# Attention's product of softmax weights and rows of h, in three float32r passes for one graph of each pair

## The chip, the cores and the metric

The kernel runs on one core of one Trainium2 chip. The metric is the device time of one execution in microseconds (us); lower is better. The kernel before takes 2072.49 us, the median of 4 runs (2069.57 to 2074.41).

## The reference

There are 64 graphs of 256 nodes with 256 features, each with its own 256x256 adjacency matrix. Layer 0 is a gated graph network: three rounds of message passing and a GRU cell. Layer 1 is a graph attention layer. Both are preceded by a layer norm and a ReLU and followed by a residual sum.

```python
# layer 0
h = jnp.maximum(_layernorm(x), 0.0)
for i in range(3):
    m = einsum('bnd,de->bne', h, weight[i]);  aggr = einsum('bst,bsd->btd', A, m)
    h = _gru_cell(aggr, h, w_ih, w_hh, b_ih, b_hh)
x = x + h
# layer 1
g = jnp.maximum(_layernorm(x), 0.0)
h = einsum('bnd,od->bno', g, W)
e = (h @ a_left)[:, :, None] + (h @ a_right)[:, None, :]
e = where(adj == 0, NEG_INF, where(e > 0, e, 0.2 * e))
x = x + einsum('bij,bjd->bid', softmax(e, -1), h)
```

The kernel multiplies the softmax weights by g first and applies W afterwards; the two orders give the same result. The "rows of h" of the change are these rows g (buffer `hb` in the kernel).

## The kernel before, in words

The graphs go in 32 pairs (`G` = 2). A pair's state is held transposed, 128 features x 512 nodes (two graphs side by side) in each of two buffers. A pair runs through three GRU rounds and then through attention.

**Numbers in two forms.** Most products are made in float32r, the fast reduced form of float32 on TensorE, in three passes. `split` (lines 470 to 478) makes three float32r buffers out of one float32 buffer: one ScalarE copy with a scale (line 473) and two VectorE operations (lines 474 and 476). The first two passes go into a PSUM bank, ScalarE multiplies the bank in place by `SPLIT + 1`, and the third pass is added on top. In the gates the first two passes are line 498, the scaling line 512, the third pass line 503; in attention's product with W ("project") both matmul parts are line 778 and the scaling is line 783. Attention's first product, softmax weights by rows of `hb` ("mix", line 770), is made in plain float32 instead: four matmuls with 256 columns for each graph, which the trace records as eight MATMULs.

**Attention, for all pairs but the last** (`far`): rows of scores are masked, their exponentials taken (line 753), the weights turned by the DMA engines into `pT` (line 536 joins the two halves on ScalarE: "p copy"), mixed on TensorE into the bank `pg`, split ("c0", "c1"), projected, and added to the residual (line 787). The last pair has an attention of its own (lines 793 and after), row block by row block.

**Buffers.** Every tile comes from a class of equal slots: 25 `full` (float32), 32 `round` (float32r) of 128x512, 8 PSUM banks and a few small ones.

**The order of the work.** A planner (`Plan.run`) writes out one static order for each engine before anything runs. Each operation has an engine, an estimated time for which it occupies the engine, a latency, and the buffers that it reads and writes. The planner walks through time: of all operations whose inputs and buffers are there it places the one that can start first, and among equals the one with the smallest priority value. That value comes from the deadline of the pair, less the latencies of what follows, less an entry of the table `LEAD` (in ns), which moves an operation by name ahead (positive) or back (negative). `WINDOW` = 4 pairs may be under way at once. Names get the prefix "first", "late" or "last" for the pairs 0, 30 and 31. At run time each engine goes through its list in order, and semaphores hold it where an input is not there yet.

TensorE therefore finds work of two or three pairs in its list, interleaved: gates of one pair beside the products of another's attention.

Of the kernel before, what the change touches and what calls it, by code (L numbers as in the profile page):

```python
# [10 lines left out]
F32 = mybir.dt.float32  # L11
# [3 lines left out]
AF = mybir.ActivationFunctionType  # L15
ALU = mybir.AluOpType
# [8 lines left out]


LEAD = {
    "w load": 17000, "w d": -3000, "G": 4000, "first A": 32000, "first in 0 eps": 5000, "first nh 1 topF": 4000,
    "first lo 1": -14000, "in 0 eps": -2000, "in 0 relu": 71000, "in 1 stats": -3000, "in 1 relu": 57000,
    "h0 0": 3000, "h1 1": -8000, "prop 0": 4000, "g0 0": -24000, "g0 1": -19000, "prop 1": 30000, "g1 1": 23000,  # L30
    "r 0 topT": 2000, "ni 0 topF": -18000, "ni 0 scale": -10000, "u add 0": 1000, "z 0 topF": -114000,
    "z 0 rest": 11000, "z 0": 55000, "d add 0": -14000, "r 1 topT": -55000, "r 1 rest": -22000, "nh 1 rest": 5000,
    "ni 1 topF": -23000, "z 1 topF": -162000, "z 1 scale": -94000, "z 1": 51000, "d sub 1": -3000,
    "d add 1": -14000, "back copy 1": -43000, "mask 0": -6000, "mid 1 stats": -52000, "max 1": -19000,
    "c0 0": 12000, "late r 0 rest": -15000, "late nh 0 rest": -22000, "late r 1 topF": 16000,
    "late r 1 rest": -3000, "late nh 1 topF": 15000, "late ni 1 topF": -8000, "late project 1 scale": -47000,
    "last in 0 stats": 10000, "last in 1 relu": 16000, "last h0 1": -30000, "last h1 1": 21000,
    "last r 0 topF": -2000, "last nh 0 rest": 2000, "last z 0 rest": -36000, "last lo 0": -47000,
    "last back 1": -34000, "last nh 0 of 0 topF": 20000, "last ni 1 of 0 rest": 12000,
    "last nh 0 of 1 topF": -17000, "last nh 1 of 1 topF": 21000,  # L40
}


# [164 lines left out]
def tile_gated_gnn_then_gat(  # L208
# [39 lines left out]
    nc = tc.nc  # L248
    P = 128
    B, N, D = x.shape  # L250
    L = weight.shape[0]
    NB = N // P
    DB = D // P
    G = 2
# [20 lines left out]
    ALL = (0, 1)  # L275
    ONE = (0,)

    def parts(b):
        return b.t[:, :GN].rearrange("p (k d) -> p k d", k=2)
# [3 lines left out]
    def pe(name, n, fn, **kw):  # L283
        return plan.op(name, "PE", n, n + 220, fn, **kw)

    def act(name, n, fn, **kw):
        plan.op(name, "ACT", n, n + 170, fn, **kw)

    def dve(name, n, fn, **kw):
        plan.op(name, "DVE", n, n + 160, fn, **kw)  # L290

    def dve2(name, n, fn, **kw):
        plan.op(name, "DVE", n, n + 160, fn, port=True, **kw)
# [8 lines left out]
    MM, TR, PROP, PASS = 432, 109, 120, 232  # L302
    A512, V512, S512, VP256, C512 = 475, 605, 660, 392, 522
    LINE, SPREAD = 4600, 4600
    SPLIT = 4096.0
    C = 1.0 / SPLIT
    BELOW = 1.0 - C / 2
# [162 lines left out]
    def split(name, v, bank=False):  # L470

        v0, v1, vd = Buf("round"), Buf("round"), Buf("round")
        act(name + " 0", A512 if bank else C512, lambda: nc.scalar.activation(v0.t, v.t, AF.Copy, scale=BELOW), r=[(v, ALL)], w=[(v0, ONE)])  # L473
        (dve if bank else dve2)(name + " 1", V512, lambda: nc.vector.tensor_sub(v1.t, v.t, v0.t.bitcast(F32)),  # L474
                                r=[(v, ALL), (v0, ONE)], w=[(v1, ONE)])
        dve2(name + " d", V512, lambda: nc.vector.scalar_tensor_tensor(  # L476
            vd.t, v1.t.bitcast(F32), -SPLIT, v0.t.bitcast(F32), op0=ALU.mult, op1=ALU.add),
            r=[(v0, ONE), (v1, ONE)], w=[(vd, ONE)])
        return v0, v1, vd
# [5 lines left out]
    def columns(part):  # L485
        return slice(part[0] * N, (part[-1] + 1) * N)
# [47 lines left out]
    def join(name, src, dst, order="b j n"):  # L534

        act(name, 1065, lambda: nc.scalar.copy(  # L536
            dst.t.bitcast(U16).rearrange("p (j n b) -> p j n b", j=2, b=2),
            src.t.bitcast(U16).rearrange(f"p ({order}) -> p j n b", j=2, b=2)), r=[(src, ALL)], w=[(dst, ALL)])

    def planes(b):  # L540
        return lambda rows: b.t[rows].bitcast(U16).rearrange("p (b k n) -> p b k n", b=2, n=P)
# [27 lines left out]
    def pair(p):  # L569
# [5 lines left out]
        A = [Buf("round") for _ in range(G)]  # L575
        h = [Buf("full") for _ in range(G)]
        hi, lo = [Buf("round") for _ in range(G)], [Buf("round") for _ in range(G)]
        for g in range(G):
            dve2("A", 340, lambda g=g: nc.vector.tensor_scalar(A[g].t, ADJ[p][g].t, 0.0, None, op0=ALU.not_equal),
                r=[(ADJ[p][g], ALL)], w=[(A[g], ONE)])  # L580
# [3 lines left out]
                r=[(h[g], ALL), (hi[g], ONE)], w=[(lo[g], ONE)])  # L584
# [21 lines left out]
        for i in range(L):  # L606
            last = i == L - 1
# [23 lines left out]
            for part in [(0,), (1,)] if apart else [ALL]:  # L631
                cols, of = columns(part), " of %d" % part[0] if apart else ""
                for db in range(DB):
                    plan.due = 1000.0 * SLOT * (3 * p + 2 * i) + (8000.0 * part[0] if apart else 0)
                    d = hT[db]
                    pr = gate(f"r {db}{of}", db, [("hh", hs), (i, gs)], tops, True, part=part)
                    r_, z_, u = Buf("full"), Buf("full"), Buf("full")
                    act(f"r {db}{of}", fit(575, part), lambda b=r_, k=pr, db=db, cols=cols: nc.scalar.activation(  # L638
                        b.t[:, cols], k.t[:, cols], AF.Tanh, bias=b_rz[:, db : db + 1], scale=0.5),
                        r=[(pr, ONE), ("b_rz", ONE)], w=[(r_, ONE)])  # L640
# [12 lines left out]
                        r=[(pz, ONE), ("b_rz", ONE)], w=[(z_, ONE)])  # L653
# [10 lines left out]
            if not last:  # L664
                hi, lo = [Buf("round") for _ in range(DB)], [Buf("round") for _ in range(DB)]
            for g, db in [(g, db) for g in range(G) for db in range(DB)] if apart else []:
                hn = Buf("bank")

                def back(g=g, db=db, hn=hn):
# [6 lines left out]
                    r=[(hn, ALL)], w=[(XR[g], ALL)])  # L676
            for db in range(0 if apart else DB):
# [12 lines left out]
                if last:  # L690
                    for g in range(G):
                        v = lambda b, g, db: b.t.rearrange("p (g k f) -> p g k f", g=G, k=NB)[:, g]
                        dve_(f"res {db}", 335, lambda g=g, db=db, b=XR[g], hn=hn, v=v: nc.vector.tensor_add(
                            parts(b)[:, :, ts(db, P)], parts(b)[:, :, ts(db, P)], v(hn, g, db)), r=[(hn, ALL)], w=[(XR[g], ALL)])
                else:
                    act(f"hi {db}", C512, lambda b=hi[db], hn=hn: nc.scalar.copy(b.t, hn.t), r=[(hn, ALL)], w=[(hi[db], ONE)])
                    dve_(f"lo {db}", V512, lambda b=hi[db], c=lo[db], hn=hn: nc.vector.tensor_sub(c.t, hn.t, b.t.bitcast(F32)),  # L697
                         r=[(hn, ALL), (hi[db], ONE)], w=[(lo[db], ONE)])
# [3 lines left out]
        hb, sc, pm_ = ([Buf("full") for _ in range(G)] for _ in range(3))  # L702
# [5 lines left out]
        for g in range(G):  # L708
# [4 lines left out]
            for nb in range(NB):  # L713
                for n in range(2):
                    c = 12 + n * NB + nb
# [3 lines left out]
                        r=[(hb[g], (nb,)), ("va", ONE)], w=[(sm, (c,)), (sc[g], (nb,))])  # L719
# [3 lines left out]
            if p < NPAIR - 1:  # L723
# [3 lines left out]
                    r=[(sm, (14, 15))], w=[(line, ONE)])  # L727
# [13 lines left out]
            for nb in range(NB):  # L741
# [4 lines left out]
                r=[(A[g], ONE), (sc[g], ALL)], w=[(pm_[g], ALL)])  # L746
            dve(f"max {g}", 610, lambda b=pm_[g], sm=sm: nc.vector.tensor_reduce(sm.t[:, 0:NB], parts(b), AX.X, ALU.max, negate=True),
                r=[(pm_[g], ALL)], w=[(sm, ONE)])
# [9 lines left out]
        for g in range(G if far else 0):  # L758
            sm = sms[g]
            dve("recip", 70, lambda sm=sm: nc.vector.reciprocal(sm.t[:, 8 : 8 + NB], sm.t[:, 4 : 4 + NB]),  # L760
                r=[(sm, (1,))], w=[(sm, (2,))])
            pT, pg, pv = Buf("full"), Buf("bank"), Buf("bank")
            rs = Buf("full")
            dma_turn(f"p turn {g}", pm_[g], pT, [((rs, ALL), planes(rs), slice(None))])
            join(f"p copy {g}", rs, pT)

            def mix(g=g, pT=pT, pg=pg):
                for db in range(DB):
                    for jb in range(NB):
                        nc.tensor.matmul(pg.t[:, ts(db, N)], parts(hb[g])[:, jb, ts(db, P)],  # L770
                                         pT.t.rearrange("p (i j n) -> p i j n", j=NB, n=P)[:, :, jb, :], start=(jb == 0), stop=(jb == NB - 1))

            pe(f"mix {g}", 4 * MM, mix, r=[(pT, ALL), (hb[g], ALL)], w=[(pg, ONE)])
            cs = split(f"c{g}", pg, True)

            def project(js, first, cs=cs, pv=pv):
                for n, (ib, db, j) in enumerate((ib, db, j) for ib in range(NB) for db in range(DB) for j in js):
                    nc.tensor.matmul(pv.t[:, ts(ib, D)], cs[j].t[:, db * N + ib * P : db * N + (ib + 1) * P],  # L778
                                     fac["W"][:, j, db, :], start=(first and n == 0), stop=True, skip_group_check=True)

            pe(f"project {g}", 8 * PROP, lambda project=project: project((0, 1), True),
               r=[(cs[0], ONE), (cs[1], ONE), ("facW", ((0, 0), (1, 0)))], w=[(pv, ONE)])
            act(f"project {g} scale", A512, lambda pv=pv: nc.scalar.activation(pv.t, pv.t, AF.Copy, scale=SPLIT + 1.0), w=[(pv, ONE)])
            pe(f"project {g} rest", 4 * PROP, lambda project=project: project((2,), False),
               r=[(cs[2], ONE), ("facW", ((0, 1), (1, 1)))], w=[(pv, ONE)])
            for nb in range(NB):
                dve(f"out {g}", VP256, lambda b=XR[g], nb=nb, pv=pv, sm=sm: nc.vector.scalar_tensor_tensor(
                    parts(b)[:, nb, :], pv.t[:, ts(nb, D)], sm.t[:, 8 + nb : 9 + nb], parts(b)[:, nb, :],
                    op0=ALU.mult, op1=ALU.add), r=[(pv, ONE), (sm, (2,))], w=[(XR[g], (nb,))])
            dma("store", 256, lambda g=g, b=XR[g]: nc.sync.dma_start(rows(out, G * p + g), parts(b)), r=[(XR[g], ALL)])  # L790


        for g, ib in [(g, ib) for g in range(G) for ib in range(NB)] if not far else []:
            stagger(g)
            sm, name, row, total = sms[g], f" {g} {ib}", (sms[g], (("row", ib),)), (sms[g], (("total", ib),))
            pt, pT, pg, ag, pv = Buf("bank"), Buf("full"), Buf("bank"), Buf("full"), Buf("bank")
# [4 lines left out]
                r=[row], w=[total])  # L801
# [17 lines left out]
            def project(ag=ag, pv=pv):  # L819
# [6 lines left out]
                r=[(pv, ONE), total], w=[(XR[g], (ib,))])  # L826
# [39 lines left out]
```

## Time and profile before

| what | value |
|---|---|
| median of 4 runs | 2072.49 us |
| the profiled execution, its own time | 2073.07 us |
| its span in the profile | 2071.3 us |
| granted TensorE clock | 0.998 |
| busy: TensorE / weight load / VectorE / ScalarE / GpSimd | 99% / 82% / 84% / 85% / 8% |
| mean DMA rate | 117 GB/s |

"PE" is TensorE's matmul row, "PEld" its weight loads, "DVE" VectorE, "ACT" ScalarE, "POOL" GpSimd, "SP" the engine that issues the DMAs. A group row gives line, engine, operation, destination and source tiles, shape, the count, the busy time, and the mean duration of one instruction in ns; what follows the last bar is the idle time of the engine ahead of these instructions and what ended it. A duration holds the whole instruction; queued instructions of one engine overlap a little, so the step from one start to the next is shorter. In the chain of waits a piece is a start, a length and what ran; the length is the step by which the chain moved on.

### The profile page before, as it was taken

The page shows a single profiled execution, that of the slowest core. Times are in us where ns is not written, and L with a number is a line of the kernel's source. Part 1 is how long each engine was busy: PE and PEld are TensorE (multiplying, and loading weights), DVE is VectorE, ACT ScalarE, POOL GpSimd, SP SyncE. Part 2 cuts the span into 40 slices and gives each one's busy share as a digit, 9 for nine tenths or more (in the row PEclk, how much of TensorE's full clock was granted, in tenths as well). Part 3 has the DMA queues.
Part 4 walks back from the last instruction along what each step waited for, and adds up shares of the span by engine and source line. Part 5 has one row for each costly group of instructions (what it writes and reads, how often), then busy time and mean ns, then how long its engine had stood idle before and what let it go on. Part 6 is the DMA issues. An engine that isn't in the chain of part 4 may idle for free.

```text
span 2071.3 us, 31400 instructions
## 1 busy us (share of the span) xinstructions
PE 2048.3 (99%) x9957; PEld 1693.9 (82%) x9957; DVE 1738.2 (84%) x3892; ACT 1761.8 (85%) x3049; POOL 157.7 (8%) x198
## 2 busy tenths in 40 slices
PE   8999999999999999999999999999999999999997
PEld 6888887888888888888888888888888888888887
DVE  7778888888888888888788888788888888888877
ACT  6788888888888888988888888888888888888876
POOL 1000000000000000000000000000000000000000
PEclk9999999999999999999999999999999999999999
DMA  4257677667776566866677766778766778666632
GB/s 121 62 100 131 128 136 107 119 108 133 138 119 112 114 122 128 140 112 109 110 135 130 126 114 115 113 130 143 110 114 119 121 128 143 108 116 111 111 70 57
DMA packets 742918, 241.52 MB, mean 117 GB/s; under 512 B 666704, under 2 KB 742752, under 8 KB 742752
## 3 DMA queue, kind: packets, MB, share of 16 engines
q1 hardware_dynamic: 742720, 239.51, 66.0%
q8 instruction: 78, 1.28, 0.3%
q14 instruction: 88, 0.72, 0.2%
q10 hardware_dynamic: 32, 0.01, 0.0%
HBM read 61.09 MB, written 16.84 MB: 38 GB/s over the span
## 4 chain that ended last, share of the span: by engine, by line
PE 86%; DVE 5%; DMA 4%; ACT 3%; issue 1%; SPq 0%; ACTq 0%; DVEq 0%
PE bank L498 46%; PE bank L503 23%; PE bank L619 8%; PE bank L778 4%; DMA full<-full 4%; PE bank L770 4%; DVE round L474 1%; PE bank L447 1%; ACT full L564 1%; ACT full L536 1%; DVE round L476 1%; ACT bank L512 0%; ACT round L473 0%; DVE full L745 0%; DVE full L657 0%
## 5 line engine op out<-in xcount | busy, mean ns | idle before, releaser
L498 PE MATMUL bank<-round,fac 128*128 128x512 f32 (+1 forms) x2328 | 617.1, 393 | 0.3
L498 PE MATMUL bank<-round,fac_hh 128*128 128x512 f32 (+1 forms) x2328 | 613.1, 396 | 0.0
L498 PEld LDWEIGHTS bank<-round,fac 128*128 128x128 f32 x2328 | 433.2, 188 | 105.8 <-DVE round L474 2.8
L498 PEld LDWEIGHTS bank<-round,fac_hh 128*128 128x128 f32 x2328 | 430.6, 188 | 96.7
L512 ACT ACTIVATE bank<-bank 128x512 f32<-128x512 f32 (+1 forms) x582 | 334.1, 577 | 95.5 <-PE bank L498 88.0
L536 ACT COPY full<-full 128x1024 uint16<-128x1024 uint16 x308 | 358.6, 1165 | 31.8 <-DMA full<-full 24.4
L503 PE MATMUL bank<-round,fac 128*128 128x512 f32 (+1 forms) x1164 | 356.5, 392 | 0.0
L503 PE MATMUL bank<-round,fac_hh 128*128 128x512 f32 (+1 forms) x1164 | 353.8, 394 | 1.1 <-ACT bank L512 1.1
L476 DVE SCALAR_TENSOR_TENSOR round<-round,round 128x512 fp32r<-128x512 f32 x446 | 305.9, 688 | 8.0
L503 PEld LDWEIGHTS bank<-round,fac 128*128 128x128 f32 x1164 | 215.1, 188 | 55.0 <-ACT bank L512 5.5
L558 POOL TENSOR_TENSOR small<-small,nhalf 128x2 f32<-128x2 f32 x128 | 123.8, 975 | 1690.3 <-DVE small L556 1613.4
L503 PEld LDWEIGHTS bank<-round,fac_hh 128*128 128x128 f32 x1164 | 205.9, 188 | 46.0 <-ACT bank L512 8.9
L474 DVE TENSOR_TENSOR round<-bank,round 128x512 fp32r<-128x512 f32 x254 | 173.8, 686 | 60.2 <-ACT round L473 56.9
L619 PEld LDWEIGHTS bank<-round,round 128*128 128x128 f32 x1536 | 208.7, 191 | 14.2 <-DVE round L697 0.3
L619 PE MATMUL bank<-round,round 128*128 128x256 f32 x1536 | 215.7, 284 | 0.1
L643 DVE SCALAR_TENSOR_TENSOR full<-full,bank 128x512 f32<-128x512 f32 (+1 forms) x194 | 131.5, 678 | 54.4 <-ACT full L638 52.7
L648 ACT ACTIVATE full<-full,vec 128x512 f32<-128x512 f32 (+1 forms) x194 | 139.4, 719 | 41.9 <-DVE full L646 21.5
L651 ACT ACTIVATE full<-bank,b_rz 128x512 f32<-128x512 f32 (+1 forms) x194 | 132.7, 684 | 45.9 <-PE bank L503 44.5
L473 ACT ACTIVATE round<-bank 128x512 fp32r<-128x512 f32 x254 | 146.7, 592 | 28.7 <-PE bank L619 25.9
L657 DVE SCALAR_TENSOR_TENSOR full<-full,full 128x512 f32<-128x512 f32 (+1 forms) x194 | 130.4, 672 | 32.1 <-ACT full L651 31.9
L474 DVE TENSOR_TENSOR round<-full,round 128x512 fp32r<-128x512 f32 x192 | 130.7, 683 | 30.0 <-ACT round L473 27.6
L646 DVE TENSOR_TENSOR full<-full,bank 128x512 f32<-128x512 f32 (+1 forms) x194 | 131.0, 676 | 24.7 <-PE bank L503 17.3
(95 smaller groups left out, 2295.6 us busy)
## 6 DMA issues: line engine op xcount, KB each, us to landing
full<-full SPq DMA_DIRECT2D x492, 128.0 KB, 3.7
x<-in_x_dram SPq DMA_DIRECT2D x64, 256.0 KB, 3.2
adj<-in_adj_dram SPq DMA_DIRECT2D x64, 256.0 KB, 4.3
full<-in_x_dram SPq DMA_DIRECT2D x64, 256.0 KB, 3.3
full<-full SPq DMA_DIRECT2D x248, 64.0 KB, 2.5
out_dram<-full SPq DMA_DIRECT2D x62, 256.0 KB, 2.5
full<-line SPq DMA_DIRECT2D x62, 128.0 KB, 3.8
full<-full SPq DMA_TRANSPOSE x308, 3.2
```

The costliest lines, as they stand in the source:

```text
L473: act(name + " 0", A512 if bank else C512, lambda: nc.scalar.activation(v0.t, v.t, AF.Copy, scale=BELOW), r=[(v, ALL)], w=[(v0, ONE)])
L474: (dve if bank else dve2)(name + " 1", V512, lambda: nc.vector.tensor_sub(v1.t, v.t, v0.t.bitcast(F32)), r=[(v, ALL), (v0, ONE)], w=[(v1, ...
L476: dve2(name + " d", V512, lambda: nc.vector.scalar_tensor_tensor(vd.t, v1.t.bitcast(F32), -SPLIT, v0.t.bitcast(F32), op0=ALU.mult, op1=ALU ...
L498: nc.tensor.matmul(bank.t[:, cols], f(m, j, kb), b.t[:, cols], start=(first and n == 0), stop=True, skip_group_check=True)
L503: nc.tensor.matmul(bank.t[:, cols], f(m, 2, kb), s[kb][2].t[:, cols], start=False, stop=True, skip_group_check=True)
L512: act(name + " scale", fit(575 if "nh" in name else 515, part), lambda: nc.scalar.activation(bank.t[:, cols], bank.t[:, cols], AF.Identity ...
L536: act(name, 1065, lambda: nc.scalar.copy(dst.t.bitcast(U16).rearrange("p (j n b) -> p j n b", j=2, b=2), src.t.bitcast(U16).rearrange(f"p ...
L619: nc.tensor.matmul(pa.t[:, ts(g, N)], b, parts(A[g])[:, sb, :], start=(n == 0), stop=(n == len(terms) - 1))
L643: dve(f"u {db}{of}", fit(S512, part), lambda u=u, k=ph, b=r_, cols=cols: nc.vector.scalar_tensor_tensor(u.t[:, cols], b.t[:, cols], 1.0, k ...
L646: dve(f"u add {db}{of}", fit(V512, part), lambda u=u, k=pn, cols=cols: nc.vector.tensor_add(u.t[:, cols], u.t[:, cols], k.t[:, cols]), r=[ ...
L648: act(f"tanh {db}{of}", fit(615, part), lambda u=u, en=en, cols=cols: nc.scalar.activation(u.t[:, cols], u.t[:, cols], AF.Tanh, bias=b_i[: ...
L651: act(f"z {db}{of}", fit(575, part), lambda b=z_, k=pz, db=db, cols=cols: nc.scalar.activation(b.t[:, cols], k.t[:, cols], AF.Tanh, bias=b ...
```

## The change

For graph 0 of each pair from 0 to 30, the mix is made in three float32r passes like the other products. Both operands are split: `hb` into three buffers `w` (scaled by `C * BELOW`, one ScalarE and two VectorE operations), `pT` into three buffers `vs` (the same counts). Eight matmuls of 256 columns go into `pg`, ScalarE scales the bank, four more matmuls follow. Graph 1 keeps the four float32 matmuls, and the last pair is as before. The table `LEAD` is another one: 30 entries in place of 60, 16 names in both.

```diff
 LEAD = {
-    "w load": 17000, "w d": -3000, "G": 4000, "first A": 32000, "first in 0 eps": 5000, "first nh 1 topF": 4000,
-    ...
-    "last nh 0 of 1 topF": -17000, "last nh 1 of 1 topF": 21000,
+    "w load": 18000, "first h0 d": -14000, "first nh 1 topF": 3000, "first ni 1 topF": 11000, "in 0 stats": 5000,
+    "in 0 eps": 4000, "in 1 stats": 19000, "in 1 shift": -113000, "in 1 relu": 75000, "h0 1": -9000,
+    "nh 0 topF": 9000, "ni 0 topF": -33700, "ni 0 rest": -10000, "z 0 topF": -125000, "z 0 rest": 40000,
+    "d mul 0": 20000, "d add 0": 8000, "r 1 topT": -93000, "ni 1 topF": -33300, "z 1 topF": -182000,
+    "z 1 scale": -142000, "back copy 1": -41000, "mid 0 stats": -18000, "mid 1 stats": -102000, "c1 0": 72000,
+    "late nh 1 topF": 15000, "late back 0 gather": 15000, "late mix 0": -7000, "last in 1 stats": -18000,
+    "last back 1 of 0": 15000,
 }
...
+            def mix_in_three(first, cs, pg=pg):
+                for n, (db, jb, (w, v)) in enumerate((db, jb, c) for db in range(DB) for jb in range(NB) for c in cs):
+                    nc.tensor.matmul(pg.t[:, ts(db, N)], parts(w)[:, jb, ts(db, P)],
+                                     v.t.rearrange("p (i j n) -> p i j n", j=NB, n=P)[:, :, jb, :],
+                                     start=(first and n == 0), stop=True, skip_group_check=True)
...
-            pe(f"mix {g}", 4 * MM, mix, r=[(pT, ALL), (hb[g], ALL)], w=[(pg, ONE)])
+            if g > 0:
+                pe(f"mix {g}", 4 * MM, mix, r=[(pT, ALL), (hb[g], ALL)], w=[(pg, ONE)])
+            else:
+                w = [Buf("round") for _ in range(3)]
+                act(f"hb{g} 0", C512, lambda g=g, w=w: nc.scalar.activation(w[0].t, hb[g].t, AF.Copy, scale=C * BELOW),
+                    r=[(hb[g], ALL)], w=[(w[0], ONE)])
+                dve2(f"hb{g} 1", V512, lambda g=g, w=w: nc.vector.scalar_tensor_tensor(
+                    w[1].t, w[0].t.bitcast(F32), -SPLIT, hb[g].t, op0=ALU.mult, op1=ALU.add),
+                    r=[(hb[g], ALL), (w[0], ONE)], w=[(w[1], ONE)])
+                dve2(f"hb{g} d", V512, lambda w=w: nc.vector.tensor_sub(w[2].t, w[1].t.bitcast(F32), w[0].t.bitcast(F32)),
+                     r=[(w[0], ONE), (w[1], ONE)], w=[(w[2], ONE)])
+                vs = split(f"p{g}", pT)
+                pe(f"mix {g}", 8 * PROP, lambda cs=list(zip(w, vs)), mix=mix_in_three: mix(True, cs[:2]),
+                   r=[(b, ONE) for b in w[:2] + list(vs[:2])], w=[(pg, ONE)])
+                act(f"mix {g} scale", 515, lambda pg=pg: nc.scalar.activation(pg.t, pg.t, AF.Copy, scale=SPLIT + 1.0), w=[(pg, ONE)])
+                pe(f"mix {g} rest", 4 * PROP, lambda cs=list(zip(w, vs)), mix=mix_in_three: mix(False, cs[2:]),
+                   r=[(w[2], ONE), (vs[2], ONE)], w=[(pg, ONE)])
```

## The prediction

> **What bounds the kernel now.** I read the page first: the busy row, the 40 slices and the shares of the chain that ended last.
>
> ```profile
> span 2071.3 us, 31400 instructions
> PE 2048.3 (99%) x9957; PEld 1693.9 (82%) x9957; DVE 1738.2 (84%) x3892; ACT 1761.8 (85%) x3049; POOL 157.7 (8%) x198
> PE   8999999999999999999999999999999999999997
> PEclk9999999999999999999999999999999999999999
> PE 86%; DVE 5%; DMA 4%; ACT 3%; issue 1%; SPq 0%; ACTq 0%; DVEq 0%
> ```
>
> TensorE's row is full in all slices but the first and the last, at full clock. A matmul's duration (393 ns for 512 columns) is longer than its step, so this share alone proves little. I therefore went to the chain of waits in order of time around one attention (1048.89 to 1061 us); each piece's length is the time by which the chain moved on.
>
> ```profile
> 1048.89 0.96 PE bank L619 x8
> 1049.85 3.45 PE bank L770 x16
> 1053.30 1.86 PE bank L498 x8
> 1055.16 0.95 PE bank L778 x8
> 1056.12 0.93 PE bank L498 x4
> 1057.04 1.43 PE bank L778 x12
> ```
>
> Every piece starts where the one before ended, all on TensorE. This is streaming, not waiting: 512 columns of float32r take 1.86/8 = 0.233 us, 256 columns 1.43/12 = 0.119 us, and a float32 record 3.45/16 = 0.216 us. Table of windows of 40 us: TensorE is idle 6.8 us before 80 us (the weights), 5.4 us between 80 and 1960 us, 10.8 us after (the last pair's latencies): 23 us in all, the span less 2048.3. So a nanosecond taken from TensorE's stream in the middle is a nanosecond off the span, as long as ScalarE and VectorE go on delivering.
>
> The Trainium skill (Perfetto Trace Analysis, Identifying the Most-Contended Engine) speaks against this reading: matmul busy time is a bad measure, weight-load share a good one, and that is 82% here, with four more loads per changed graph. If TensorE had 18% to spare, the 9.2 us below would drop out and only the added waits remain, about +2.5 us. The gapless pieces decide for me.
>
> Next the groups by form, for the prices, and what TensorE's weight loads (the head of its queue) waited for between 100 and 1940 us (us in total, times, longest).
>
> ```profile
> L473 ACT ACTIVATE round<-full 128x512 fp32r<-128x512 f32 x192 | 119.4, 624 | 3.2 <-DVE full L659 3.0
> L783 ACT ACTIVATE bank<-bank 128x512 f32<-128x512 f32 x62 | 36.0, 581 | 1.4 <-PE bank L778 1.4
> L476 DVE SCALAR_TENSOR_TENSOR round<-round,round 128x512 fp32r<-128x512 f32 x446 | 305.9, 688 | 8.0
> L474 DVE TENSOR_TENSOR round<-full,round 128x512 fp32r<-128x512 f32 x192 | 130.7, 683 | 30.0 <-ACT round L473 27.6
> ```
> ```profile
> PEld bank L503 <- ACT bank L512: 11.4, 63, 0.6
> PEld bank L770 <- ACT full L536: 6.1, 11, 1.0
> PEld bank L778 <- DVE round L474: 4.8, 11, 0.5
> PEld bank L778 <- ACT bank L783: 3.3, 16, 0.2
> PEld bank L498 <- DVE round L474: 2.8, 9, 0.6
> ```
>
> These waits are short, and most are covered by the matmul still streaming: TensorE's own idle time in that stretch is 2.4 us ahead of L770, 1.4 us ahead of L778 and 0.4 us ahead of L503.
>
> **The change part by part.** *Streaming, on the path.* Graph 0's eight float32 records go: 3.45/2 = 1.725 us. Twelve float32r matmuls of 256 columns come: the project of one graph has the same count and width, 0.95 + 0.47 = 1.42 us, or 1.43 in one piece. Saved 0.30 us a graph, 31 graphs: **-9.2 us**. The trace has no float32r matmul that reads its moving rows in two stretches of 128, as the new ones do; in float32 the stretched L770 (3.45/16) and the plain L821 of the last pair (1.73/8) step alike at 0.216 us, so I take no price; a doubled step would be 31 x 12 x 0.119 = +44 us.
>
> The Trainium skill counts true float32 as four passes (FP8 and Floating Point Precision, TensorE Precision Notes) and a stream of N columns as N/2.4 + 2.5 ns (TensorE: Matmul & The Clock Gate, Back-to-back issue gap). An estimate from these is 16 x 0.109 against 12 x 0.109 us, 0.44 us a graph and -13.5 us in all. The rows have the four passes (1.725 us) but 0.119 us for a short float32r step, so I stay with 9.2.
>
> *ScalarE and VectorE, beside TensorE.* Per pair ScalarE gets two splits' first copies and a scaling, 2 x 0.624 + 0.581 = 1.83 us; VectorE four operations of 0.683 to 0.688, 2.74 us. For 31 pairs that is 57 and 85 us: ScalarE 1762 to 1819 (88%), VectorE 1738 to 1823 (88% of a span near 2065). Both stay below the span, so neither becomes the bound by its sum. Cover: they run while TensorE streams the gates of other pairs. If all cover were gone, the cost would be 57 + 85 = 142 us. What counts is what stands behind them in line: on ScalarE the gates' scalings L512, on which L503 waits; on VectorE the splits L474, on which L498 and L778 wait. ScalarE has 3049/32 = 95 instructions a pair and VectorE 122, so three and four more are 3%. By proportion the 11.4 + 2.8 us of queue waits grow by 0.5 us; I take 1.5, as fuller engines wait more than in proportion, with bounds of 0 and 142.
>
> *New waits on TensorE.* The mix had one entry, behind the "p copy" (L536). It gets two: behind the split of `pT`, then behind its own scaling. Queued behind each stand gates of other pairs, which wait along. Nearest rows: L778 has just these two kinds; its queue waits 4.8 + 3.3 us fall on 58 graphs (29 pairs in 1840 us), so 31 graphs pay 4.3 us, or 0.7 by TensorE's own idle 1.4 us. What goes is half of L770's: 3.2 us by the queue, 1.3 by TensorE. Net +1.1 by the queue, -0.6 by TensorE; bounds -3.2 (old wait gone, none new) and +4.3 (all new, nothing gone). I take the queue's: **+1.0**.
>
> *Latency and buffers.* `pg` passes one split, a scaling and a third pass more, some 0.62 + 0.69 + 0.58 + 0.47 = 2.4 us, before "c0". Only that graph's project and store come later, and other pairs' gates fill in. The bank is held 1 to 2 us longer; counted along the planner's order of before, at most 8 of 8 banks are held, but 4 in the median. `round` holds at most 31 of 32 (median 21, 95% at 27); up to six more can make the planner put something off, at nothing where a gate can stand in. `full` (up to 24 of 25) gains, since `hb[0]` comes free once split. I take 0; the upper bound is in the queue term. No DMA is added or passed by an added instruction on SP; POOL gets none.
>
> *The table.* With other `LEAD` values many operations change places, in the first and last pairs too. The trace can't price an order that it doesn't have. What can be won is part of 23 us of idle, of which the 5.4 in the middle are the movable part; what can be lost is of the same size as all of it. I take 0, with -4 and +12.
>
> *Sum:* -9.2 + 1.5 + 1.0 = -6.7. The profiled execution took 2073.07 (span 2071.3 and 1.8 around it), 0.6 above the median; the median goes to 2072.49 - 6.7 = **2065.8 us**.
>
> **The rivals.** A measurement here can tell about 0.2% (4.1 us): faster is below 2068.3, slower above 2076.6.
>
> *Forecast, 0.55:* TensorE stays gapless; own range 2062 (all of 9.2 and 1.3 from a better order) to 2068.3.
>
> *The waits take it back, 0.17:* the new entries cost 4.3 by the queue and the added instructions 3: -9.2 + 7.3 = -1.9, 2070.6. For it: L778 already waits at 27 of its entries. Against it: TensorE itself stood only 1.4 us there.
>
> *Slower: ScalarE and VectorE hold up the gates, 0.22.* Place: in-order lists in the stretch after the attention (1045 to 1062 us), where ScalarE is busy 15.0 of 17 us and VectorE 13.9 already. Price: a share of the 142 us. It breaks even at 9.2/142 = 6.5% and is slower beyond (9.2 + 4.1)/142 = 9.4%; at 15% it is +21.3 - 9.2 = +12.1, 2084.6. For it: 85% and 84% are averages, and `round` is near its limit. Against it: TensorE's 5.4 us of idle in the middle are 0.2% of what both engines do there now.
>
> *The passes don't stream at 0.119, 0.03:* at a doubled step -9.2 + 44 = +35, 2107.
>
> *The table alone costs more than the passes save, 0.03:* +12 in the first and last pairs with the waits above, 2078.
>
> Faster 0.55, same 0.17, slower 0.22 + 0.03 + 0.03 = 0.28. The range 2062 to 2084 leaves out some 0.06 below, and above it half of the third case and the fourth: 0.2 together.
>
> **What would show it.** L770's records fall from 496 to 248; a new line of matmuls with 372 records steps at 0.119 us, 1.42 a graph. ScalarE's busy time rises by some 57 us, VectorE's by 85. Idle of TensorE between 80 and 1960 us stays under 9 us. I am wrong if that idle passes 14 us with ACT L512 or DVE L474 as what ended it (the slower rival), if the new matmuls' step isn't 0.119 us (the streaming term), or if the difference lies before 80 or after 1960 us (the table).

## The result, and the profile after

The changed kernel takes 2077.51 us (median of 39 runs, 2070.95 to 2082.01) against 2071.98 us for the kernel before (58 runs). The ratio is 1.0024 with a 95% interval of 1.0019 to 1.003: slower, by 4 to 6 us. The forecast was 2065.8, faster by 6.7; the miss is 11.7 us. The profiled execution took 2079.46 us, 2077.6 of them span, 6.3 more than before.

The page's span, busy row and shares of the chain that ended last:

```profile
span 2077.6 us, 31649 instructions
PE 2043.6 (98%) x10081; PEld 1688.7 (81%) x10081; DVE 1805.5 (87%) x4016; ACT 1795.6 (86%) x3142; POOL 144.8 (7%) x198
PE 76%; DMA 10%; ACT 8%; DVE 3%; SPq 1%; issue 1%; ACTq 0%; DVEq 0%
```

TensorE is busy 4.7 us less and idle 11.0 us more (34.0 in place of 23.0). The chain now runs through TensorE for 76% of the span, not 86%; DMA and ScalarE have taken 11 points. The added instructions are all there: 93 on ScalarE, 124 on VectorE, 31 times three and four. Their busy rows grew by 34 and 67 us, not by 57 and 85, because the durations of queued instructions overlap and a busy row counts the overlap once.

Did the passes stream as priced? The chain through one attention, and the two groups:

```profile
1050.94 0.95 PE bank L763 x8
1051.89 1.86 PE bank L492 x8
1053.75 0.48 PE bank L763 x4
1054.23 0.96 PE bank L613 x8
1055.19 1.73 PE bank L770 x8
```
```profile
L763 PE MATMUL bank<-round,round 128*128 128x256 f32 x372 | 55.2, 283 | 0.0
L770 PE MATMUL bank<-full,full 128*128 128x256 f32 x248 | 60.3, 386 | 7.3 <-ACT full L530 7.0
```

Yes: 372 records on the new line 763, 0.95 + 0.48 = 1.43 us for a graph, against 1.73 for the float32 product that graph 1 keeps. No idle time stands in front of line 763. The stretched moving rows cost nothing.

Windows of the profiled execution (us of the window; then busy us by engine, TensorE first; the last figures are the granted clock, the DMA share and GB/s), and below them the middle window of the kernel before:

```profile
0.00:80.00 80.00, 72.94 (x333) 55.97 (x334) 59.10 (x127) 51.82 (x97) 7.34 (x18) 1.00 0.35 94
80.00:1960.00 1880.00, 1867.28 (x9176) 1543.73 (x9176) 1657.18 (x3668) 1662.58 (x2880) 132.67 (x174) 1.00 0.66 121
1960.00:2077.60 117.60, 103.40 (x574) 89.00 (x573) 89.18 (x224) 81.17 (x166) 4.84 (x6) 0.93 0.34 63
```
```profile
80.00:1960.00 1880.00, 1874.63 (x9069) 1551.26 (x9068) 1599.52 (x3560) 1632.08 (x2794) 145.77 (x175) 1.00 0.70 121
```

TensorE's idle time is 7.1 us up to 80 us (6.8 before), 12.7 in the middle (5.4) and 14.2 at the end (10.8). What ended the idle time in the middle:

```profile
PE bank L770 <- ACT full L530: 6.5, 9, 1.1
PE bank L497 <- ACT bank L506: 5.5, 10, 1.0
```

What its load queue waited for between 100 and 1940 us:

```profile
PEld bank L497 <- ACT bank L506: 33.2, 133, 1.4
PEld bank L770 <- ACT full L530: 9.4, 13, 1.3
PEld bank L763 <- ACT bank L787: 1.4, 4, 0.4
```

The mix's new entries cost almost nothing (line 763, 1.4 us behind its scaling). What grew are waits that were there before: the gates' third passes behind their scalings (11.4 to 33.2 us, 63 to 133 times), and graph 1's float32 mix behind its "p copy" (6.1 to 9.4, though it has half the entries).

Each pair's first project matmul can be found in the trace, and the steps from one to the next show where the time lies. The last column is from the 28th pair's project to the end, the tail. Every row is one profiled execution, and executions of one kernel differ by several us; that of the last row but one was the slowest of its six. The rows below "changed" belong to the experiments further down.

| kernel | first project at | mean step of 27 | shortest step | 28th to the end |
|---|---|---|---|---|
| before | 172.8 | 62.93 | 62.35 | 199.4 |
| changed | 172.6 | 63.01 | 62.13 | 203.7 |
| changed order, float32 product, no load | 172.2 | 63.15 | 62.43 | 202.0 |
| changed order, three passes, no load | 172.8 | 63.00 | 62.14 | 199.3 |
| before, searched table | 171.1 | 62.60 | 62.39 | 196.8 |
| changed, second table | 174.8 | 62.77 | 62.17 | 198.2 |
| order of the second table, three passes, no load | 173.8 | 62.53 | 62.17 | 196.8 |
| order of the second table, float32 product, no load | 173.9 | 62.76 | 62.42 | 195.7 |

An undisturbed pair is 0.22 us shorter than before; against the float32 product at the same order (62.43) it is 0.30 us shorter, just what the passes were priced at. The mean pair is 0.08 us longer than before, so waits grew from 0.58 to 0.88 us a pair. 27 x 0.08 = 2.2 us come from the middle and 4.3 from the tail.

TensorE's steps, from one matmul's start to the next, say the same. With each kind of matmul at its median step, the 27 pairs hold about 1677 us of streaming and 22 us of longer steps before, 1669 and 32 after.

### The profile page after: what moved, and what is told of

Same layout as the page of the kernel before. It is cut to its first block, busy times and chain, and to the rows that moved or that the text cites. A ratio compares the mean times of both kernels' runs of the same rounds, so it can differ in the third digit from the quotient of the medians.

```text
span 2077.6 us, 31649 instructions
## 1 busy us (share of the span) xinstructions
PE 2043.6 (98%) x10081; PEld 1688.7 (81%) x10081; DVE 1805.5 (87%) x4016; ACT 1795.6 (86%) x3142; POOL 144.8 (7%) x198
## 4 chain that ended last, share of the span: by engine, by line
PE 76%; DMA 10%; ACT 8%; DVE 3%; SPq 1%; issue 1%; ACTq 0%; DVEq 0%
PE bank L492 39%; PE bank L497 20%; DMA full<-full 7%; PE bank L613 7%; PE bank L794 4%; PE bank L770 3%; ACT full L530 2%; DMA full<-line 2%; ACT bank L506 1%; PE bank L763 1%; SPq L522 1%; ACT full L558 1%; DMA line<-small 1%; PE bank L441 1%; ACT round L467 1%
## 5 line engine op out<-in xcount | busy, mean ns | idle before, releaser
L506 ACT ACTIVATE bank<-bank 128x512 f32<-128x512 f32 (+1 forms) x582 | 336.3, 581 | 90.1 <-PE bank L492 88.5
L530 ACT COPY full<-full 128x1024 uint16<-128x1024 uint16 x308 | 358.3, 1169 | 35.6 <-DMA full<-full 31.9
L470 DVE SCALAR_TENSOR_TENSOR round<-round,round 128x512 fp32r<-128x512 f32 x477 | 321.3, 685 | 4.8 <-PE bank L492 0.6
L552 POOL TENSOR_TENSOR small<-small,nhalf 128x2 f32<-128x2 f32 x128 | 110.9, 868 | 1482.6 <-DVE small L550 1482.0
L468 DVE TENSOR_TENSOR round<-full,round 128x512 fp32r<-128x512 f32 x223 | 150.3, 686 | 73.5 <-ACT round L467 73.4
L613 PEld LDWEIGHTS bank<-round,round 128*128 128x128 f32 x1536 | 203.3, 191 | 10.4 <-DVE round L691 1.0
L649 DVE TENSOR_TENSOR full<-full,full 128x512 f32<-128x512 f32 (+1 forms) x194 | 131.9, 681 | 48.6 <-ACT full L642 48.4
L467 ACT ACTIVATE round<-full 128x512 fp32r<-128x512 f32 x223 | 138.6, 623 | 16.6 <-DVE full L653 16.5
L642 ACT ACTIVATE full<-full,vec 128x512 f32<-128x512 f32 (+1 forms) x194 | 139.0, 717 | 14.8 <-DVE full L640 14.8
```

The lines of the kernel that those rows point to most:

```text
L506: act(name + " scale", fit(575 if "nh" in name else 515, part), lambda: nc.scalar.activation(bank.t[:, cols], bank.t[:, cols], AF.Identity ...
L530: act(name, 1065, lambda: nc.scalar.copy(dst.t.bitcast(U16).rearrange("p (j n b) -> p j n b", j=2, b=2), src.t.bitcast(U16).rearrange(f"p ...
L613: nc.tensor.matmul(pa.t[:, ts(g, N)], b, parts(A[g])[:, sb, :], start=(n == 0), stop=(n == len(terms) - 1))
L642: act(f"tanh {db}{of}", fit(615, part), lambda u=u, en=en, cols=cols: nc.scalar.activation(u.t[:, cols], u.t[:, cols], AF.Tanh, bias=b_i[: ...
L649: dve2(f"d sub {db}{of}", fit(V512, part), lambda u=u, d=d, cols=cols: nc.vector.tensor_sub(d.t[:, cols], d.t[:, cols], u.t[:, cols]), r=[ ...
```

## The experiments

**Passes, load and order, taken apart at the changed kernel's order.** The planner still sees all operations of the change and writes the same order; only what is issued differs. "Load" is the added work of ScalarE and VectorE. The kernel before ran beside every group of experiments (2071.1 to 2072.4 us); the ratios here and below, as 95% intervals, are to it.

```diff
# neither; passes only: the load goes
- activation(w[0].t, hb[g].t, ...)                 + activation(w[0].t[:, :16], hb[g].t[:, :16], ...)
- activation(v0.t, v.t, ...)                       + activation(v0.t[:, :16], v.t[:, :16], ...)
- hb 1, hb d, p 1, p d (VectorE), mix scale        + nothing issued
# neither; load only: the passes go
- mix_in_three (8 + 4 float32r matmuls)            + four float32 matmuls on w[k], vs[k]
```

> Base of a two by two at one fixed order: the order of the changed kernel, line for line, on every engine. Left out of the computation: the splits of hb and of pT for graph 0 (only 16 columns of their first copies are made, so that the product still waits for pT), the scaling and the third pass; the product is four plain float32 matmuls on these buffers. So neither the added engine work nor the three passes is there, only the other order. Theory A (thin slack: the order of the changed kernel, not the load of its added instructions, makes TensorE wait): slower than the changed kernel by most of the 9.2 us of streaming, near 2083 us, since the waits stay. Theory B (the load: seven added instructions on ScalarE and VectorE hold up the gates' scalings and splits): the waits go, the streaming of before comes back, near 2072 us.

> The same fixed order with the twelve float32r matmuls in place, but their operands cut short as in the first of these runs (16 columns of the first copies, the four VectorE operations and the scaling left out; those parts of the computation are missing). The passes without the load. Theory A: the passes give their 9 us but the waits stay: 2074 to 2077 us, hardly better than the changed kernel. Theory B: the waits go and the passes give their 9 us: 2062 to 2064 us.

> The same fixed order with all six split operations and the scaling in place, but the product as four plain float32 matmuls on one buffer of each split and no third pass (that part of the computation is left out). The load without the passes. Theory A and theory B both expect slower than the changed kernel by the passes' streaming, 9.2 us, near 2086 us; A expects it close to the run with neither (within 3 us), B expects it 12 us or more above that run.

| at the changed kernel's order | float32 product | three passes |
|---|---|---|
| without the load | 2081.3 (ratio 1.0034 to 1.0061) | 2076.3 (1.0009 to 1.0034) |
| with the load | 2082.6 (1.0042 to 1.0073) | 2077.5 (1.0019 to 1.003) |

The passes are worth 5.0 us without the load and 5.1 with it. The load costs 1.2 to 1.3 us. Each of these differences is known to some 3 us (the run with the passes alone ranged from 2070.7 to 2082.8 us): what the passes give is clear of zero, what the load costs is not. The order alone costs 2081.3 - 2071.6 = 9.7 us (7 to 12.6 by the interval). The work in it is that of before, but for 62 copies of 16 columns on ScalarE, 0.2 us each; TensorE never stood idle ahead of the product that reads them. The sum 9.7 - 5.0 + 1.2 = 5.9 is the changed kernel against the same 2071.6. In the trace of the run with neither, the order's cost lies in the middle (27 x 0.22 = 5.9 us) and in the tail (2.6).

Theory A as to the order is right. That the passes would give all of 9 us is not, and the run with the load alone came out under the 2086 that both theories expected. With the passes TensorE's idle time in the middle rises from 9.5 to 12.0 us, so part of what they free becomes waiting. The middle window of the run with neither, then of the passes alone:

```profile
80.00:1960.00 1880.00, 1870.46 (x9047) 1544.36 (x9046) 1588.17 (x3545) 1625.43 (x2847) 132.56 (x174) 1.00 0.65 121
```
```profile
80.00:1960.00 1880.00, 1867.97 (x9183) 1545.52 (x9182) 1592.81 (x3556) 1628.66 (x2853) 132.50 (x174) 1.00 0.65 121
```

The waits of the third passes stay when the load is gone, here in the run with neither, 80 to 1960 us (34.3 in 139 in the changed kernel over the same window):

```profile
PEld bank L497 <- ACT bank L506: 31.2, 136, 1.4
```

**The table alone.** Only the `LEAD` table of the kernel before is replaced by that of the change.

> The kernel before with the LEAD table of the changed kernel and nothing else: the table alone. If a table can be carried from one set of operations to another, it would lie within 15 us of before (2060 to 2087 us). If the table belongs to the exact set of operations, it loses far more than the three passes could win: over 2100 us, with TensorE idle in every pair. Either way it tells how much of the time is order.

2172.91 us, 101 us slower. A table belongs to the exact set of operations, so "the table alone" can't be had by a swap; the runs at a fixed order above are the clean form.

**Why is the order slower? Two guesses that failed.** First SP's queue: in the changed kernel it stands 193.5 us at the broadcast of the right-hand scores, which waits for the line's landing.

```diff
- pR.t[:, :N] <- line.t.to_broadcast([P, N])       # the line stored just before
+ pR.t[:, :N] <- still.to_broadcast([P, N])        # a line stored once at the start
```

> The changed kernel in its own fixed order, but the broadcast of the right-hand scores reads a line in DRAM that was written once at the start, not the line just stored (the right-hand scores are left out of the result that way). The broadcast no longer waits at the head of SP's queue for the line's landing; it and all DMAs behind it can go up to 5 us earlier. In the changed kernel that wait is 193.5 us in 58 turns, before it is 62.0 us in 33. Theory Q (the new order makes SP's queue stand, the transposes behind it come late, and TensorE waits for what they bring): 5 us or more faster than the changed kernel, 2072 us or less. Theory S (the scalings of the gates stand without slack ahead of their third passes): within 2 us of the changed kernel, 2076 to 2079 us.

> The same edit in the kernel before, as the control: the broadcast reads the line written at the start. Theory Q expects a small gain, under 2.5 us (2069.5 to 2072), since SP's queue stands there only a third as long; theory S expects none. A gain as large as in the changed kernel would say that the shorter way of the scores helps any order and explains no difference between the two.

The changed kernel went to 2079.85 (1.0028 to 1.0058), no gain, though SP's wait for the line was gone: theory Q gets no support. The queue as a whole was relieved of less: it stood longer at its transposes instead, 202.9 us against 90.4 behind one VectorE operation that feeds them. The control took 2130.02 us, 58 us more, and nobody had expected that. Its landing time, that of the kernel before, and what ScalarE waited for in the control:

```profile
full<-still SPq DMA_DIRECT2D x62, 128.0 KB, 6.9
```
```profile
full<-line SPq DMA_DIRECT2D x62, 128.0 KB, 3.8
```
```profile
ACT full L749 <- DMA full<-still: 55.7, 28, 2.5
```

The broadcast of the fixed line lands in 6.9 us (median) where that of the fresh line took 3.8; in the changed kernel it is 5.6 against 4.2. Line 749, the leaky ReLU, stands in ScalarE's list where the result used to be there in time (1.0 us of waiting in the kernel before). Now ScalarE stops for 2 us in each of 28 pairs, and everything behind it comes late. So the edit swapped one wait for a later landing and settles theory Q only in part. It does show what a static order pays when one DMA of each pair lands late.

Then the slack of the gates' scalings. The planner of the changed kernel puts the third pass of 132 gates less than 50 ns behind the end of its scaling.

```diff
- activation(bank[:, 0:512], bank[:, 0:512], Identity, bias, scale=SPLIT + 1)
+ activation(bank[:, 0:16], bank[:, 0:16], ...)    # for the 132 tight gates, or for 132 with the most slack
```

> The changed kernel in its own fixed order; the scalings of the 132 gate products whose third pass the planner put less than 50 ns behind the scaling's end are made on 16 of the 512 columns (the rest of the scaling is left out). Theory S: the waits of the third passes on ScalarE (34 us at the head of TensorE's load queue in the middle stretch) fall by over half and the time falls by 5 us or more, to 2072 or less. Theory Q: the waits fall but the time moves by under 2.5 us, as TensorE then waits for the same late pair elsewhere: 2075 to 2078 us.

> Control of the run before: the same number of scalings, 132, made on 16 columns, but those whose third passes the planner put farthest behind. ScalarE gets the same 50 to 60 us of relief. Theory S: under 2 us faster than the changed kernel, 2075.5 to 2078 us. Theory Q and the theory that plain load on ScalarE is the cause: as fast as the run with the tight ones short, within 1.5 us.

With the tight ones short: 2075.02 (1.0005 to 1.0024). With the slack ones short: 2071.57 (0.9989 to 1.0012), the larger gain. The load queue's waits, tight first, then slack:

```profile
PEld bank L508 <- ACT bank L519: 14.8, 25, 1.9
```
```profile
PEld bank L508 <- ACT bank L519: 32.8, 134, 1.5
```

The tight ones' waits went from 34.3 to 14.8 us and the time moved by 2.5 us; the other run kept them and gained 5.9, though it relieved ScalarE of less (its busy time fell by 42 us, with the tight ones short by 51). Theory S falls. These short waits are mostly covered by the matmul that still streams: with the tight ones short TensorE's own idle time behind the scalings was hardly less than the 5.5 us of the changed kernel.

```profile
PE bank L508 <- ACT bank L519: 5.2, 9, 1.5
```

The larger gain of the slack ones fits neither theory and is not explained. The biggest row of a list of waits was not the one to remove.

**Results that come by DMA.** Each join behind a DMA turn takes half of its data, so that the turn's result is ready some 0.5 us earlier. Theory L is that an order loses time where such results land too close ahead of the work that needs them.

```diff
- dst as uint16 (1024 elements) <- src as uint16 (1024)
+ dst as float32 (512 elements) <- the upper uint16 of each number in src (512)
```

> The changed kernel in its own fixed order, but each of the 308 joins behind a DMA turn (ScalarE, 1.17 us each) takes one half of its data (512 elements in place of 1024; the other halves of the numbers are left out), so that what comes by DMA is ready about 0.5 us earlier, and ScalarE is relieved by about 160 us. Theory L: 2057 to 2066 us, a gain of 11 us or more, larger than the gain of the same edit in the kernel before by 4 us or more, so that the two kernels meet or change places. If the lateness of DMA results has no part in the difference, both gain alike (within 2 us) and the changed kernel stays 4 to 7 us behind.

> The same edit in the kernel before, in its own fixed order, as the control: theory L expects 2062 to 2068 us, a gain of 4 to 9 us, since its order left more time ahead of the joins' readers. The rival expects the same gain as in the changed kernel within 2 us.

2062.67 (0.9944 to 0.997) and 2059.20 (0.9928 to 0.9956): gains of 14.8 and 13.2 us, alike within 2 us, and the changed kernel stays 3.5 behind. This is the rival's outcome, but for 3.5 in place of the 4 to 7 it named. How much of the gain is the earlier result and how much the relief of ScalarE, whose busy time fell by 139 and 151 us, is not separated. Shorter joins are worth 13 to 15 us to either kernel, but they don't tell the two apart. Neither do collisions with the loads:

```diff
- load of x, adj: 256 columns
+ from the second pair on: 16 columns
```

> The changed kernel in its own fixed order; the loads of x and of the adjacency move 16 of 256 columns from the second pair on (the rest of the tiles keeps an earlier pair's values, so those inputs are left out). SP issues the same DMAs in the same order, but some 31 MB of 241 MB are gone, and with them what a turn can collide with. Theory C (the changed kernel's order puts turns beside loads, the turns land late, in-order queues stand): a gain of 8 us or more, 2070 us or less, and larger than the same edit's gain in before by 4 us or more. If collisions with these loads have no part, both gain alike within 2 us.

> The same edit in the kernel before, in its own fixed order, as the control. Theory C: a gain of 4 us at most, 2068 to 2072 us. The rival: the same gain as in the changed kernel within 2 us.

2078.24 (1.0022 to 1.0041) and 2070.07 (0.9986 to 1.0003): both within 1.1 us of where they were (the kernel before took 2071.1 beside them). Theory C falls.

**Other orders.** The tables were searched (some 500 entries each) for the length of the planner's own order when it is replayed with late DMAs; only `LEAD` differs.

> The kernel before with another LEAD table and nothing else. The table was searched for one goal: the length of the planner's order when it is replayed with every DMA landing up to 0.6 us later than planned, drawn at random, and a few ns more for each ScalarE and VectorE operation. Theory L (an order loses time where results that come by DMA land too close ahead of the work that needs them, and the changed kernel's order has more such places): 2050 to 2060 us. If the order of before is already as good as orders get (the loss is in the load, or in the passes), it stays within 4 us of before or is slower.

> The changed kernel (three passes for graph 0, all added instructions) with a LEAD table from the same search. Theory L: the order was the loss, so the time falls well under the changed kernel and under before: 2055 to 2066 us. If the added instructions or the passes themselves cost the time, no order gets it under before: 2072 us or more.

> The changed kernel with a second LEAD table from a longer search with the same goal as the earlier one (replayed with late DMAs it is now as short as the table that gave the kernel before 2060.8 us). If the passes and their load are good for 4 us under a good order: 2054 to 2062 us, level with or under 2060.8. If the added work makes any order fragile on the chip: 2066 us or more, still behind the kernel before with its table.

> The kernel before with another table of the same search, one whose replay with late DMAs is 14 us longer than that of the table which gave 2060.8 us. If the replay with late DMAs says what the chip does: near 2070 us, between 2066 and 2075. If the gain of the first table was luck: no relation, and anything from 2058 to 2085.

| | table as given | searched table | second table |
|---|---|---|---|
| before (float32) | 2072.0 | 2060.8 (0.9934 to 0.9959) | 2066.4 (0.997 to 0.9992) |
| changed (three passes, load) | 2077.5 | 2074.9 (1.0008 to 1.0029) | 2069.2 (0.9982 to 0.9999) |

The kernel before with the searched table is the fastest complete kernel of the study, 11 us under the kernel before by order alone, and 17 under the changed one:

```profile
span 2058.2 us, 31352 instructions
PE 92%; DMA 3%; ACT 2%; DVE 1%; issue 1%; SPq 0%; ACTq 0%; DVEq 0%
```

Its chain runs through TensorE for 92%, and its mean pair is 0.21 us over its shortest. Theory L nearly held for it (0.8 us above its range) and missed for the changed kernel, whose first searched order came out 9 us above the upper end of what was expected. The second table of the kernel before came out 4 us faster than the replay suggested: the replay ranks orders, it doesn't time them.

**The same two by two at the second table's order.**

> The changed kernel at the fixed order of its second table (2069.2 us), with the twelve float32r matmuls kept and the load cut away as before: 16 columns of the first copies, the four VectorE operations and the scaling left out. If the load itself costs little and the order is what counts: within 2.5 us of 2069.2, that is 2066.7 to 2069.5. If the load is what makes the searched orders lag behind those without the passes: 2061 to 2064 us.

> The same fixed order with four plain float32 matmuls in place of the twelve and the load cut away in the same manner, so that only the order is left. If the passes are worth the same as at the first order, 5 us more than the run with the passes alone: 2071 to 2075 us. If the whole of the streaming shows in this better order: 8 to 9.2 us more.

Passes without the load 2057.61 (0.9919 to 0.9943), neither 2065.11 (0.9961 to 0.9982), all of the change 2069.2. Both are faster than had been expected. Here the passes are worth 7.5 us, nearer to the 8 to 9.2 than to the 5, and the load costs 11.6, where at the first order its cost was not clear of zero. TensorE's row of the middle window with the load and without it:

```profile
80.00:1960.00 1880.00, 1868.99 (x9194) 1543.50 (x9193) 1663.06 (x3685) 1662.45 (x2887) 134.35 (x176) 1.00 0.66 121
```
```profile
80.00:1960.00 1880.00, 1875.23 (x9225) 1550.67 (x9225) 1606.08 (x3590) 1635.35 (x2867) 134.32 (x176) 1.00 0.66 121
```

Idle 11.0 us against 4.8, and what ended it is this, with the load and without:

```profile
PE bank L609 <- ACT bank L618: 7.1, 12, 0.9
```
```profile
PE bank L609 <- ACT bank L618: 0.8, 3, 0.5
```

That is the slower rival's mechanism, the gates' scalings held up on ScalarE, at a share of 11.6/142 = 8% of the added work. It accounts for 6.3 of the 8.8 us between the two spans (2067.6 and 2058.8); the profiled run without the load was the slowest of its kernel.

## Why the prediction was wrong, step by step

- **Streaming, -9.2.** The step was right (0.119 us, 1.43 a graph, nothing for stretched rows, 0.30 us off an undisturbed pair). Its weight in the time was not: 5.0 us at the changed order and 7.5 at the other. I took TensorE's stream as the whole path because no gap showed. But a busy row has short waits inside it, since a matmul's duration is 393 ns and its step 233: the mean pair of before was 0.58 us over its shortest, some 16 us in 27 pairs, where the idle row showed 5.4. What the passes free is partly passed to these waits: at the changed order, without the load, they take about 8 us of streaming out of the 27 pairs, and the longer steps grow from 27 to 31 us.
- **The table, taken as 0 with -4 and +12.** This is the step that failed. It measured +9.7 at equal work, near the end that I had kept for the range, and the largest part of the miss of 11.7 us (4.2 are the passes' weight). The reason I gave, that an order not in the trace can't be priced, is a reason for a wide range and not for a 0. I gave "the table alone costs more than the passes save" a chance of 0.03. I placed that cost in the first and last pairs; at equal work 5.9 us of it lie in the middle and 2.6 in the tail, and the first 80 us don't show it. That rival's 2078 is close to the 2077.5 measured partly by luck: its +12 was too much, and its -9.2 as well.
- **ScalarE and VectorE, taken as 1.5, and the new waits, +1.0.** Together 2.5 against 1.2 to 1.3 at this order, which is not clear of zero. The new entries cost almost nothing, as the queue of line 763 shows. At the second order the same load cost 11.6. So the price of such a load isn't a number of the load. A likely reading, not shown beyond these two orders, is that the added work hides where the order already makes TensorE wait, and shows where the order is good.
- **The rivals.** The slower one named the right engines and the right lines (L512, now L506, ahead of the third passes), but in the result itself the load is some 1.2 us; the waits on these lines came with the order (12.1 us before, 31.2 at the changed order without the load, 34.3 with it, all from 80 to 1960 us). That the waits would take the gain back (2070.6) was too mild.
- **The Trainium skill's rule** (Perfetto Trace Analysis, Identifying the Most-Contended Engine) that matmul busy time is a bad measure spoke against my reading. It was right that 99% hides waits. What I drew from it, that the passes would then give nothing, was not: they gave 5.0 and 7.5 us. The estimate of 13.5 us from four passes and N/2.4 + 2.5 ns was farther off than the row's 9.2. That formula (TensorE: Matmul & The Clock Gate, Back-to-back issue gap) is given there for an isolated matmul, not for a stream of them with weight loads.
- **The signs that I had named.** Idle in the middle was 12.7 us, between the 9 and the 14 I had set, ended by ACT L506 (5.5) and L530 (6.5); the tail added 3.4.

**What stays open.** That the changed kernel's order is slower at equal work is shown. Which of its places makes it so is not: SP's stand at the broadcast was tested only in part, the joins' latency and the loads don't tell the two orders apart, and the tight scalings are worth less than those with slack. What the load does to a searched order is shown for one order only.

## What to carry to other kernels

In a kernel whose order is planned ahead, a change of the arithmetic and a change of the order are two changes: measure them apart by keeping the planned order and changing what is issued. Price an added load on in-order engines by the order it will stand in, not by its sum, and keep for a re-made order a term as large as all the waits in the trace, the short ones inside the busy row included (mean step less shortest step of a repeated stage). A list of waits tells where an engine stood, not what the time would be without it.

## What the runs showed of the hardware

Broadcasting one line of DRAM to 128 partitions landed in 6.9 us (median) in one kernel and 5.6 in the other when all 62 broadcasts read the same old line, against 3.8 and 4.2 when each read a line that had just been stored. The broadcasts of the old line also went out earlier, without waiting for the store; which of the two made them land later is not known. Cutting the columns of the x and adjacency loads from 256 to 16 moved neither kernel by more than 1.1 us.
